# A gated recurrence of 512 steps: PSUM banks of equal width, and the state update as one scan over h, n, h

## The chip, the cores and the metric

The kernel runs on one core of a Trainium2 chip. The metric is the device time of one execution in microseconds (us); the time before is the median of three runs. The profile is of one further execution.

## The reference

A gated recurrent layer with a residual. For each of T = 512 steps, batch 8, width 512:

```python
def step(h, x_t):
    fused = jax.nn.sigmoid(jnp.concatenate([x_t, h], axis=-1) @ w_W + w_b)
    hidden_state, output_state = jnp.split(fused, 2, axis=-1)
    memory_state = x_t @ wx_W + wx_b + hidden_state * (h @ wh_W + wh_b)
    h_new = output_state * h + (1.0 - output_state) * jnp.tanh(memory_state)
    return (h_new, h_new)
```

The output is x plus all the h_new. In what follows r is `hidden_state`, z is `output_state`, hh is `h @ wh_W + wh_b`, n is the tanh. All is fp32. Each step needs h of the step before, so the 512 steps form one chain.

## The kernel before, in words

**Layout.** On TensorE the state is the stationary operand: a tile `hT` holds 128 partitions x 32 rows (4 steps of batch 8) for one of four k-blocks, and only the eight rows of the step at hand are not zero, so that four steps accumulate into one bank, each in its own rows. The 512 outputs are split into four strips j of 128 units, one to each 32-partition column strip of the array; within a strip the 128 units are half A (64) and half B (64). The width of a matmul is then the number of columns that a bank holds: hh, z and r of one half have 64 each. `hT` exists for each half, in eight buffers (`NH`); k-blocks 0 and 1 come from hTA, 2 and 3 from hTB.

**Banks.** Bank A has hh, z and r of half A (192 columns), Z has z of half B (64), B has r and hh of half B (128); each exists twice, one set for each group of four steps (`GS`). The share of x is computed a group ahead: one k-block of 384 columns in each step goes into `xp` ("prefill", `take(pre, 1)`), from where ScalarE copies the parts into the banks of the next group (`spread`), and VectorE turns x's share of the memory state (`turn_x`). `seed` copies the bias into `xp`. In the last eight steps there is no prefill.

**Order.** From the line `ctx.enter_context(tc.manual_schedule())` on, the instructions of each engine stand in the order in which the program writes them, and each engine works through its own in order. On TensorE that is `ORDER`, a letter for the bank and a digit for the k-block, four strips each, then the prefill block. A step of hTA can be used by A0, B0 and A1 ahead of hTB, which A2 is the first to need.

**The chain of a step.** VectorE turns 32 x 32 blocks from the bank (lines 232 for r and z, 244 for hh), ScalarE takes the sigmoid of the turned r into every second element of `md0`, hh and x's share alternate in `md1`, and one scan (line 264, state = d0 * state + d1) over pairs gives r * hh + x share in every second element of `m`. ScalarE takes the tanh of that into `hd1`, VectorE puts z * h beside it (line 275, `kept`), and the second scan (line 284, `update`), with 0 and 1 - z in `hd0`, gives (1 - z) * n + z * h into the `hT` of the next step. z and 1 - z are two sigmoids of the same turned values. GpSimd adds x to the new state and writes it to the output tile (line 315); sixteen steps make one transfer out.

On VectorE the order of a step is: turn r, hh, z of A, scan A, turn hh of B, `kept` of A, turn r of B, update A, turn z of B, scan B, `kept` of B, update B, `turn_x`. The wait for the release of an `hT` buffer by GpSimd, eight steps back, hangs on the transpose of hh of half A.

Of the kernel before, what the change touches and what calls it, by code (L numbers as in the profile page):

```python
# [7 lines left out]
F32 = mybir.dt.float32  # L8
AF = mybir.ActivationFunctionType
ALU = mybir.AluOpType  # L10
PSUM = bass.MemoryType.PSUM

P = 128
NQ = 4
GS = 4
B = 8
HU = 64


DVE_FILL = 4  # L20
SYNC = mybir.DependencyInfo(mybir.DependencyClass.Sync, mybir.DependencyReason.DATA)

ORDER = "A0 B0 A1 A2 A3 B1 B2 B3 Z0 Z1 Z2 Z3"

WH = {"A": slice(0, 192), "Z": slice(192, 256), "B": slice(256, 384)}

XP = {"A": slice(0, 192), "Z": slice(192, 256), "X": slice(256, 384), "B": slice(384, 512)}


@with_exitstack  # L30
def tile_cond_rnn_residual(
# [7 lines left out]
    out: bass.AP,  # L39
    TC: int,  # L40
):

# [18 lines left out]
    nc = tc.nc  # L63
    NCH = x.shape[0]
    T = NCH * TC
    NG = T // GS

    const = ctx.enter_context(tc.tile_pool(name="const", bufs=1))
# [7 lines left out]
    def load_x(c):  # L76
        if c < NCH:
            t_ = xin_p.tile([P, NQ, TC * B], F32, tag="xin", name=f"xin_{c}")
            nc.sync.dma_start(out=t_, in_=x[c].rearrange("p (k n) -> p k n", k=NQ))
            xins[c] = t_  # L80
# [7 lines left out]
    hin = const.tile([P, NQ, B], F32, name="hin")  # L88
# [8 lines left out]
    for k in range(NQ):  # L97
# [5 lines left out]

    NH = 2 * GS
    hT = [
        [const.tile([P, 32, 2, 2], F32, name=f"hT{n}{i}") for i in range(NH)]
        for n in "AB"
    ]

    md0 = [[const.tile([P, 32, 2, 2], F32, name=f"md0{n}{i}") for i in range(2)] for n in "AB"]  # L110
    md1 = [const.tile([P, 2, 32, 2, 2], F32, name=f"md1{i}") for i in range(2)]
    hd0 = [[const.tile([P, B, 2, 2], F32, name=f"hd0{n}{i}") for i in range(2)] for n in "AB"]
    hd1 = [[const.tile([P, B, 2, 2], F32, name=f"hd1{n}{i}") for i in range(2)] for n in "AB"]
    zs = [[const.tile([P, 2, B], F32, name=f"z{n}{i}") for i in range(2)] for n in "AB"]
    zeros = const.tile([P, 512], F32, name="zeros")
    nc.vector.memset(zeros, 0.0)
    for t_ in hT[0] + hT[1]:
        nc.gpsimd.memset(t_, 0.0)
    for n, t_ in enumerate(hd0[0] + hd0[1] + md0[0] + md0[1]):
        (nc.vector if n < DVE_FILL else nc.gpsimd).memset(t_, 0.0)  # L120

    def state(hf, i):

        s = i % GS
        return hT[hf][i % NH][:, B * s : B * s + B, :, 1]

    for hf in range(2):
        nc.vector.tensor_copy(
            state(hf, 0), hin[:, 2 * hf : 2 * hf + 2].rearrange("p c b -> p b c")
        )  # L130

    banks = [
        {n: psum.tile([P, c.stop - c.start], F32, name=f"{n}{q}") for n, c in WH.items()}
        for q in range(2)
    ]
    xps = [psum.tile([P, 512], F32, name=f"xp{q}") for q in range(2)]
# [12 lines left out]

    written = {}  # L150

    def act(key, *args, **kw):
        inst = nc.scalar.activation(*args, **kw).ins  # L153
        if key in written:
            tc.declare_no_dep(inst, written[key], reason="ordered through VectorE")
        written[key] = inst

    def seed(g):

        nc.scalar.copy(xps[g % 2], bias)  # L160
# [13 lines left out]
    def spread(g, names):  # L174

        for n in names:
            nc.scalar.copy(banks[g % 2][n], xps[g % 2][:, XP[n]])

    def turn_x(g, e):

        c0 = XP["X"].start + 32 * e
        nc.vector.transpose(
            md1[g % 2][:, e // 2, :, e % 2, 1], xps[g % 2][:, c0 : c0 + 32]
        )

    def take(it, n=None):
        while n is None or n > 0:
            if next(it, it) is it:
                return
            n = None if n is None else n - 1  # L190

    for g in range(2):
        seed(g)
        take(prefill(g))
        if g == 0:
            spread(0, "ABZ")
            for e in range(NQ):
                turn_x(0, e)
            seed(0)
    ctx.enter_context(tc.manual_schedule())  # L200

    pool_done = {}
    for i in range(T):
        g, s = divmod(i, GS)
        c, t = divmod(i, TC)
        ps = banks[g % 2]
        if t == 0:
            load_x(c + 3)
            ot = out_p.tile([P, NQ, TC, B], F32, tag="ot", name=f"ot_{c}")
        if s == 0:  # L210
            pre = prefill(g + 2) if g + 2 < NG else iter(())

        for n in ORDER.split():
            bank, k = n[0], int(n[1])
            hs = hT[k // 2][i % NH][:, :, k % 2, 1]
            for j in range(NQ):
                mm(ps[bank][32 * j : 32 * j + 32, :], hs, wh[:, k, j, WH[bank]])
        take(pre, 1)

        rows = slice(B * s, B * s + B)  # L220
        def flat(t_):
            return t_.rearrange("p n c s -> p (n c s)")

        raw = {
            "h": (ps["A"][:, :HU], ps["B"][:, HU:]),
            "z": (ps["A"][:, HU : 2 * HU], ps["Z"]),
            "r": (ps["A"][:, 2 * HU :], ps["B"][:, :HU]),
        }

        def turned(n, hf):  # L230
            t_ = work.tile([P, 2, 32], F32, tag=f"t{n}{hf}", name=f"t{n}{hf}_{i}")
            nc.vector.transpose(t_.rearrange("p c n -> p (c n)"), raw[n][hf])  # L232
            return t_[:, :, rows]

        def turn_r(hf):
            act(
                ("r", hf, g % 2, s),
                md0[hf][g % 2][:, rows, :, 1].rearrange("p n c -> p c n"),
                turned("r", hf),
                AF.Sigmoid,  # L240
            )

        def turn_h(hf):
            inst = nc.vector.transpose(  # L244
                md1[g % 2][:, hf, :, :, 0].rearrange("p n c -> p c n"), raw["h"][hf]
            ).ins

            if hf == 0 and i + 1 - NH in pool_done:
                tc.add_manual_dep(inst, pool_done[i + 1 - NH].name, SYNC)

        def turn_z(hf):
            tz = turned("z", hf)
            act(("z", hf, i % 2), zs[hf][i % 2], tz, AF.Sigmoid)
            act(
                ("zc", hf, i % 2),
                hd0[hf][i % 2][:, :, :, 1].rearrange("p n c -> p c n"),
                tz,
                AF.Sigmoid,
                scale=-1.0,
            )  # L260

        def memory(hf):
            m = work.tile([P, B, 2, 2], F32, tag=f"m{hf}", name=f"m{hf}_{i}")
            nc.vector.tensor_tensor_scan(  # L264
                flat(m),
                flat(md0[hf][g % 2][:, rows]),
                flat(md1[g % 2][:, hf, rows]),
                0.0,
                ALU.mult,
                ALU.add,  # L270
            )
            act(("n", hf, i % 2), hd1[hf][i % 2][:, :, :, 0], m[:, :, :, 1], AF.Tanh)

        def kept(hf):
            nc.vector.tensor_tensor(  # L275
                hd1[hf][i % 2][:, :, :, 1],
                zs[hf][i % 2].rearrange("p c n -> p n c"),
                state(hf, i),
                ALU.mult,
            )  # L280

        def update(hf):
            s1 = (i + 1) % GS
            nc.vector.tensor_tensor_scan(  # L284
                flat(hT[hf][(i + 1) % NH][:, B * s1 : B * s1 + B]),
                flat(hd0[hf][i % 2]),
                flat(hd1[hf][i % 2]),
                0.0,
                ALU.mult,
                ALU.add,  # L290
            )

        turn_r(0)
        turn_h(0)
        turn_z(0)
        memory(0)
        turn_h(1)
        kept(0)
        turn_r(1)
        update(0)  # L300
        turn_z(1)
        memory(1)
        kept(1)
        update(1)

        if g + 1 < NG:
            turn_x(g + 1, s)
            if s == 0:
                spread(g + 1, "A")
            elif s == 1:  # L310
                spread(g + 1, "BZ")
            elif s == 3 and g + 3 < NG:
                seed(g + 3)
        for hf in range(2):
            pool_done[i + 1] = nc.gpsimd.tensor_tensor(  # L315
                ot[:, 2 * hf : 2 * hf + 2, t, :].rearrange("p c n -> p n c"),
                xins[c][:, 2 * hf : 2 * hf + 2, t * B : t * B + B].rearrange("p c n -> p n c"),
                state(hf, i + 1),
                ALU.add,
            ).ins  # L320
        if t == TC - 1:
            nc.sync.dma_start(out=out[c], in_=ot.rearrange("p k t b -> p (k t b)"))
            xins.pop(c)
# [62 lines left out]
```

## Time and profile before

| | us |
|---|---|
| median of three runs (lowest, highest) | 1721.8 (1721.33, 1722.57) |
| profiled execution, its time | 1723.64 |
| profiled execution, its span | 1721.9 |
| PE busy (modelled ends) | 1707.1 |
| DVE busy | 1138.9 |
| ACT busy | 894.6 |
| POOL busy | 254.6 |

PE is TensorE, PEld its weight loads, DVE VectorE, ACT ScalarE, POOL GpSimd. A line of the timeline has the start in us from the span's start, the duration, the engine, the line of the code, the operation, output and inputs by the names of the program (buffer numbers left out), the shape, and how many were put together; in brackets the idle time before it, and what ended that. Loads of weights run ahead of the matmuls, so idle time before a load is not yet time lost. A matmul appears twice in the records[...]. Ends of matmuls are modelled; their starts are measured. In the tile view a line has the least, the median and the largest duration in ns, the first and last start, and the shape.

### The profile page before, as it was taken

Reading aid. Unit: us, or ns where it says so; the run is one execution under the profiler, and the core shown is the slowest. Engines: PE = TensorE matmul, PEld = TensorE weight load, DVE = VectorE, ACT = ScalarE, POOL = GpSimd, SP = SyncE. Lnnn points to the kernel's source line nnn. Section 1 sums busy time; section 2 is a strip of 40 time slices with the busy share of each in tenths; the row PEclk is TensorE's granted clock in tenths of the full one; section 3 lists DMA queues with packets and bytes.
Section 4 is the critical chain, followed back from the end, with each engine's and each line's share of the span. In section 5 each row is a group of like instructions: output and inputs, shape, how many; then the busy total and the mean of one; then the engine's idle time right before and its main releaser. Section 6 shows DMA issues by size and latency. Waiting matters only on the chain.

```text
span 1721.9 us, 121031 instructions
## 1 busy us (share of the span) xinstructions
PE 1707.1 (99%) x53312; PEld 1484.6 (86%) x53312; DVE 1138.9 (66%) x6663; ACT 894.6 (52%) x4610; POOL 254.6 (15%) x1048
## 2 busy tenths in 40 slices
PE   8999999999999999999999999999999999999998
PEld 5888888888888888888888888888888888888887
DVE  3666666666666666666666666666666666666666
ACT  3555555555555555555555555555555555555554
POOL 1111111111111111111111111111111111111111
PEclk9999999999999999999999999999999999999999
DMA  4000000000000000000000000000000000000000
GB/s 180 17 5 17 17 17 16 17 4 17 17 17 17 4 17 17 17 17 4 17 17 17 17 17 5 17 17 17 17 4 17 16 17 17 5 17 11 11 11 10
DMA packets 11232, 31.09 MB, mean 18 GB/s; under 512 B 1360, under 2 KB 1360, under 8 KB 10704
## 3 DMA queue, kind: packets, MB, share of 16 engines
q1 hardware_dynamic: 10368, 23.07, 3.9%
q8 instruction: 416, 6.82, 1.6%
q14 instruction: 112, 0.92, 0.2%
q10 hardware_dynamic: 336, 0.28, 0.1%
HBM read 14.96 MB, written 8.39 MB: 14 GB/s over the span
## 4 chain that ended last, share of the span: by engine, by line
PE 98%; DMA 1%; DVE 0%; issue 0%; ACT 0%; ACTq 0%; POOLq 0%; POOL 0%
PE A L139 39%; PE B L139 25%; PE xp L139 19%; PE Z L139 14%; DMA wh<-in_wh_dram 1%; DMA bias<-in_bias_dram 0%; DVE tr L232 0%; ACT md0A L153 0%; DVE hTA L284 0%; DVE m L264 0%; DVE md L244 0%; ACTq L85 0%; POOLq L380 0%; POOL ot L315 0%; DVE hd1A L275 0%
## 5 line engine op out<-in xcount | busy, mean ns | idle before, releaser
L139 PE MATMUL A<-wh,hTA 128*32 128x192 f32 x8192 | 554.0, 326 | 2.2 <-DVE hTA L284 2.2
L139 PEld LDWEIGHTS A<-wh,hTA 128*32 128x32 f32 x8192 | 319.3, 137 | 179.7 <-DVE hTA L284 178.4
L139 PE MATMUL A<-wh,hTB 128*32 128x192 f32 x8192 | 447.4, 327 | 2.0 <-DMA wh<-in_wh_dram 2.0
L139 PE MATMUL xp<-wx,xin 128*32 128x384 f32 x4096 | 444.9, 489 | 4.5 <-ACT xp L160 4.5
L139 PE MATMUL B<-wh,hTA 128*32 128x128 f32 x8192 | 449.3, 273 | 0.0
L232 DVE STREAM_TRANSPOSE tr<-A 128x64 f32<-128x64 f32 x512 | 128.0, 250 | 470.2 <-PE A L139 470.2
L153 ACT ACTIVATE md0A<-tr 128x16 f32<-128x16 f32 x512 | 121.1, 237 | 479.7 <-DVE tr L232 479.7
L139 PEld LDWEIGHTS B<-wh,hTA 128*32 128x32 f32 x8192 | 362.4, 136 | 2.0
L139 PE MATMUL B<-wh,hTB 128*32 128x128 f32 x8192 | 336.4, 273 | 0.0
L139 PEld LDWEIGHTS A<-wh,hTB 128*32 128x32 f32 x8192 | 300.4, 137 | 36.9 <-DMA wh<-in_wh_dram 1.6
L315 POOL TENSOR_TENSOR ot<-xin,hTA 128x16 f32<-128x16 f32 x512 | 126.3, 247 | 1115.6 <-DVE hTA L284 1032.9
L139 PEld LDWEIGHTS B<-wh,hTB 128*32 128x32 f32 x8192 | 266.3, 137 | 0.0
L139 PE MATMUL Z<-wh,hTB 128*32 128x64 f32 x8192 | 240.6, 226 | 0.0
L139 PE MATMUL Z<-wh,hTA 128*32 128x64 f32 x8192 | 234.6, 223 | 0.0
L139 PEld LDWEIGHTS Z<-wh,hTA 128*32 128x32 f32 x8192 | 218.3, 141 | 0.0
L139 PEld LDWEIGHTS Z<-wh,hTB 128*32 128x32 f32 x8192 | 200.1, 148 | 0.0
L315 POOL TENSOR_TENSOR ot<-xin,hTB 128x16 f32<-128x16 f32 x512 | 125.2, 245 | 348.1 <-DVE hTB L284 342.8
L153 ACT ACTIVATE md0B<-tr 128x16 f32<-128x16 f32 x512 | 119.1, 233 | 70.7 <-DVE tr L232 0.5
L284 DVE TENSOR_TENSOR_SCAN hTB<-hd0B,hd1B 128x32 f32<-128x32 f32 x512 | 115.1, 225 | 52.9
L264 DVE TENSOR_TENSOR_SCAN m<-md0B,md 128x32 f32<-128x32 f32 x512 | 147.7, 289 | 0.0
L244 DVE STREAM_TRANSPOSE md<-B 128x64 f32<-128x64 f32 x512 | 146.8, 287 | 0.0
L153 ACT ACTIVATE zB<-tz 128x16 f32<-128x16 f32 x512 | 110.8, 216 | 53.9
(42 smaller groups left out, 1860.5 us busy)
## 6 DMA issues: line engine op xcount, KB each, us to landing
xin<-in_x_dram SPq DMA_DIRECT2D x32, 256.0 KB, 3.0
out_dram<-ot SPq DMA_DIRECT2D x32, 256.0 KB, 2.0
wx<-in_wx_dram SPq DMA_DIRECT2D x4, 768.0 KB, 7.2
wh<-in_wh_dram SPq DMA_DIRECT2D x4, 768.0 KB, 11.3
bias<-in_bias_dram ACTq DMA_DIRECT2D x4, 64.0 KB, 5.1
hin<-in_h_dram ACTq DMA_DIRECT2D x1, 16.0 KB, 8.0
```

The source lines that it names most:

```text
L139: nc.tensor.matmul(out_, lhsT, rhs, start=start, stop=False, skip_group_check=True)
L153: inst = nc.scalar.activation(*args, **kw).ins
L232: nc.vector.transpose(t_.rearrange("p c n -> p (c n)"), raw[n][hf])
L244: inst = nc.vector.transpose(md1[g % 2][:, hf, :, :, 0].rearrange("p n c -> p c n"), raw["h"][hf]).ins
L264: nc.vector.tensor_tensor_scan(flat(m), flat(md0[hf][g % 2][:, rows]), flat(md1[g % 2][:, hf, rows]), 0.0, ALU.mult, ALU.add,)
L284: nc.vector.tensor_tensor_scan(flat(hT[hf][(i + 1) % NH][:, B * s1 : B * s1 + B]), flat(hd0[hf][i % 2]), flat(hd1[hf][i % 2]), 0.0, ALU.mu ...
L315: pool_done[i + 1] = nc.gpsimd.tensor_tensor(ot[:, 2 * hf : 2 * hf + 2, t, :].rearrange("p c n -> p n c"), xins[c][:, 2 * hf : 2 * hf + 2, ...
```

## The change

Three things are changed together.

- **Banks.** R has r of both halves, G has hh and z of half A, H has z and hh of half B, all of 128 columns. The order of TensorE becomes `R0 R1 G0 G1 R2 R3 G2 G3 H0 H1 H2 H3`: four blocks with hTA ahead of the first with hTB, and H last. The weights' columns are laid out to suit.
- **Update.** `hT` has three slots an element: h, n, h. The scan of `update` reads the `hT` of this step in this order with 0, -1 and 1 - z in `hd0`: it gives h, then n - h, then h + (1 - z)(n - h), and writes all three to the `hT` of the next step, whose third slot is the new state and what TensorE loads (a stride of three slots by two instead of two by two). The tanh goes to the second slot; ScalarE copies the new state to the first slot after the updates of both halves. `kept`, `hd1`, `zs` and the sigmoid of z are gone.
- **Order and waits.** VectorE turns r of both halves first, then works half A through to its update, then half B. The transpose of z waits for the sigmoid of r of its half (so the scan needs no wait on ScalarE of its own), and the wait for GpSimd's release moves to the transpose of r of half B. The copies into the next group's banks are one bank a step. Five memsets of one column each follow `turn_x` in each step. GpSimd's two additions of a step change places: half B's first. In the setup VectorE fills 15 tiles instead of 4; hT's fills join those shared with GpSimd.

In the built program, the first scan of a half waits for VectorE's own transpose alone, the update for ScalarE alone, GpSimd's addition of half B for VectorE, and that of half A for nothing further.

```diff
-DVE_FILL = 4
+DVE_FILL = 15
+IDLE = 5
-ORDER = "A0 B0 A1 A2 A3 B1 B2 B3 Z0 Z1 Z2 Z3"
+ORDER = "R0 R1 G0 G1 R2 R3 G2 G3 H0 H1 H2 H3"
-WH = {"A": slice(0, 192), "Z": slice(192, 256), "B": slice(256, 384)}
+WH = {"G": slice(0, 128), "R": slice(128, 256), "H": slice(256, 384)}
-XP = {"A": slice(0, 192), "Z": slice(192, 256), "X": slice(256, 384), "B": slice(384, 512)}
+XP = {"G": slice(0, 128), "R": slice(128, 256), "X": slice(256, 384), "H": slice(384, 512)}
...
-        [const.tile([P, 32, 2, 2], F32, name=f"hT{n}{i}") for i in range(NH)]
+        [const.tile([P, 32, 2, 3], F32, name=f"hT{n}{i}") for i in range(NH)]
...
-    md1 = [const.tile([P, 2, 32, 2, 2], F32, name=f"md1{i}") for i in range(2)]
-    hd0 = [[const.tile([P, B, 2, 2], F32, name=f"hd0{n}{i}") for i in range(2)] for n in "AB"]
-    hd1 = [[const.tile([P, B, 2, 2], F32, name=f"hd1{n}{i}") for i in range(2)] for n in "AB"]
-    zs = [[const.tile([P, 2, B], F32, name=f"z{n}{i}") for i in range(2)] for n in "AB"]
+    md1 = [[const.tile([P, 32, 2, 2], F32, name=f"md1{n}{i}") for i in range(2)] for n in "AB"]
+    hd0 = [[const.tile([P, B, 2, 3], F32, name=f"hd0{n}{i}") for i in range(2)] for n in "AB"]
...
-    for t_ in hT[0] + hT[1]:
-        nc.gpsimd.memset(t_, 0.0)
-    for n, t_ in enumerate(hd0[0] + hd0[1] + md0[0] + md0[1]):
+    for n, t_ in enumerate(hd0[0] + hd0[1] + md0[0] + md0[1] + hT[0] + hT[1]):
         (nc.vector if n < DVE_FILL else nc.gpsimd).memset(t_, 0.0)
+    for t_ in hd0[0] + hd0[1]:
+        nc.gpsimd.memset(t_[:, :, :, 1], -1.0)
+    idle = const.tile([P, IDLE], F32, name="idle")
...
-            hs = hT[k // 2][i % NH][:, :, k % 2, 1]
+            hs = hT[k // 2][i % NH][:, :, k % 2, 2]
...
-            "h": (ps["A"][:, :HU], ps["B"][:, HU:]),
-            "z": (ps["A"][:, HU : 2 * HU], ps["Z"]),
-            "r": (ps["A"][:, 2 * HU :], ps["B"][:, :HU]),
+            "h": (ps["G"][:, :HU], ps["H"][:, HU:]),
+            "z": (ps["G"][:, HU:], ps["H"][:, :HU]),
+            "r": (ps["R"][:, :HU], ps["R"][:, HU:]),
...
         def turn_r(hf):
-            act(
+            tr, inst = turned("r", hf)
+            if hf == 1 and i + 1 - NH in pool_done:
+                tc.add_manual_dep(inst, pool_done[i + 1 - NH].name, SYNC)
+            r_done[hf] = act(
                 ("r", hf, g % 2, s),
                 md0[hf][g % 2][:, rows, :, 1].rearrange("p n c -> p c n"),
-                turned("r", hf),
+                tr,
                 AF.Sigmoid,
             )
...
         def turn_z(hf):
-            tz = turned("z", hf)
-            act(("z", hf, i % 2), zs[hf][i % 2], tz, AF.Sigmoid)
+            tz, inst = turned("z", hf)
+            tc.add_manual_dep(inst, r_done[hf].name, SYNC)
             act(
                 ("zc", hf, i % 2),
-                hd0[hf][i % 2][:, :, :, 1].rearrange("p n c -> p c n"),
+                hd0[hf][i % 2][:, :, :, 2].rearrange("p n c -> p c n"),
                 tz,
                 AF.Sigmoid,
                 scale=-1.0,
...
-            act(("n", hf, i % 2), hd1[hf][i % 2][:, :, :, 0], m[:, :, :, 1], AF.Tanh)
-
-        def kept(hf):
-            nc.vector.tensor_tensor(
-                hd1[hf][i % 2][:, :, :, 1],
-                zs[hf][i % 2].rearrange("p c n -> p n c"),
-                state(hf, i),
-                ALU.mult,
-            )
+            act(("n", hf, i % NH), state(hf, i, 1), m[:, :, :, 1], AF.Tanh)
...
                 flat(hd0[hf][i % 2]),
-                flat(hd1[hf][i % 2]),
+                flat(hT[hf][i % NH][:, rows]),
...
         turn_r(0)
+        turn_r(1)
         turn_h(0)
         turn_z(0)
         memory(0)
+        update(0)
         turn_h(1)
-        kept(0)
-        turn_r(1)
-        update(0)
         turn_z(1)
         memory(1)
-        kept(1)
         update(1)
+        for hf in range(2):
+            act(("h", hf, (i + 1) % NH), state(hf, i + 1, 0), state(hf, i + 1), AF.Copy)
 
         if g + 1 < NG:
             turn_x(g + 1, s)
-            if s == 0:
-                spread(g + 1, "A")
-            elif s == 1:
-                spread(g + 1, "BZ")
-            elif s == 3 and g + 3 < NG:
+            if s < 3:
+                spread(g + 1, "RGH"[s])
+            elif g + 3 < NG:
                 seed(g + 3)
-        for hf in range(2):
+        for n in range(IDLE):
+            nc.vector.memset(idle[:, n : n + 1], 0.0)
+        for hf in (1, 0):
             pool_done[i + 1] = nc.gpsimd.tensor_tensor(
```

More of the change, by code (lines that the diff above doesn't have):

```diff
@@ L110, in tile_cond_rnn_residual, with state @@
     md0 = [[const.tile([P, 32, 2, 2], F32, name=f"md0{n}{i}") for i in range(2)] for n in "AB"]
-    md1 = [const.tile([P, 2, 32, 2, 2], F32, name=f"md1{i}") for i in range(2)]
-    hd0 = [[const.tile([P, B, 2, 2], F32, name=f"hd0{n}{i}") for i in range(2)] for n in "AB"]
-    hd1 = [[const.tile([P, B, 2, 2], F32, name=f"hd1{n}{i}") for i in range(2)] for n in "AB"]
-    zs = [[const.tile([P, 2, B], F32, name=f"z{n}{i}") for i in range(2)] for n in "AB"]
+    md1 = [[const.tile([P, 32, 2, 2], F32, name=f"md1{n}{i}") for i in range(2)] for n in "AB"]
+    hd0 = [[const.tile([P, B, 2, 3], F32, name=f"hd0{n}{i}") for i in range(2)] for n in "AB"]
     zeros = const.tile([P, 512], F32, name="zeros")
     nc.vector.memset(zeros, 0.0)
-    for t_ in hT[0] + hT[1]:
-        nc.gpsimd.memset(t_, 0.0)
-    for n, t_ in enumerate(hd0[0] + hd0[1] + md0[0] + md0[1]):
+    for n, t_ in enumerate(hd0[0] + hd0[1] + md0[0] + md0[1] + hT[0] + hT[1]):
         (nc.vector if n < DVE_FILL else nc.gpsimd).memset(t_, 0.0)
-    def state(hf, i):
+    for t_ in hd0[0] + hd0[1]:
+        nc.gpsimd.memset(t_[:, :, :, 1], -1.0)
+    idle = const.tile([P, IDLE], F32, name="idle")
+    def state(hf, i, slot=2):
         s = i % GS
-        return hT[hf][i % NH][:, B * s : B * s + B, :, 1]
+        return hT[hf][i % NH][:, B * s : B * s + B, :, slot]
     for hf in range(2):
-        nc.vector.tensor_copy(
-            state(hf, 0), hin[:, 2 * hf : 2 * hf + 2].rearrange("p c b -> p b c")
-        )
+        for slot in (0, 2):
+            nc.vector.tensor_copy(
+                state(hf, 0, slot), hin[:, 2 * hf : 2 * hf + 2].rearrange("p c b -> p b c")
+            )
     banks = [
@@ L150, in tile_cond_rnn_residual, with act @@
     written = {}
-    def act(key, *args, **kw):
-        inst = nc.scalar.activation(*args, **kw).ins
+    def act(key, out_, in_, func, **kw):
+        inst = nc.scalar.activation(out_, in_, func, **kw).ins
         if key in written:
@@ L156, in act @@
         written[key] = inst
+        return inst
     def seed(g):
@@ L182, in turn_x @@
         nc.vector.transpose(
-            md1[g % 2][:, e // 2, :, e % 2, 1], xps[g % 2][:, c0 : c0 + 32]
+            md1[e // 2][g % 2][:, :, e % 2, 1], xps[g % 2][:, c0 : c0 + 32]
         )
@@ L195, in tile_cond_rnn_residual @@
         if g == 0:
-            spread(0, "ABZ")
+            spread(0, "RGH")
             for e in range(NQ):
@@ L231, in turned @@
             t_ = work.tile([P, 2, 32], F32, tag=f"t{n}{hf}", name=f"t{n}{hf}_{i}")
-            nc.vector.transpose(t_.rearrange("p c n -> p (c n)"), raw[n][hf])
-            return t_[:, :, rows]
+            inst = nc.vector.transpose(t_.rearrange("p c n -> p (c n)"), raw[n][hf]).ins
+            return t_[:, :, rows], inst
+        r_done = [None, None]
         def turn_r(hf):
-            act(
+            tr, inst = turned("r", hf)
+            if hf == 1 and i + 1 - NH in pool_done:
+                tc.add_manual_dep(inst, pool_done[i + 1 - NH].name, SYNC)
+            r_done[hf] = act(
                 ("r", hf, g % 2, s),
                 md0[hf][g % 2][:, rows, :, 1].rearrange("p n c -> p c n"),
-                turned("r", hf),
+                tr,
                 AF.Sigmoid,
@@ L243, in turn_h @@
         def turn_h(hf):
[L244 to L249, printed above, removed]
+            nc.vector.transpose(
+                md1[hf][g % 2][:, :, :, 0].rearrange("p n c -> p c n"), raw["h"][hf]
+            )
         def turn_z(hf):
-            tz = turned("z", hf)
-            act(("z", hf, i % 2), zs[hf][i % 2], tz, AF.Sigmoid)
+            tz, inst = turned("z", hf)
+            tc.add_manual_dep(inst, r_done[hf].name, SYNC)
             act(
                 ("zc", hf, i % 2),
-                hd0[hf][i % 2][:, :, :, 1].rearrange("p n c -> p c n"),
+                hd0[hf][i % 2][:, :, :, 2].rearrange("p n c -> p c n"),
                 tz,
@@ L266, in memory @@
                 flat(md0[hf][g % 2][:, rows]),
-                flat(md1[g % 2][:, hf, rows]),
+                flat(md1[hf][g % 2][:, rows]),
                 0.0,
@@ L271, in memory @@
             )
-            act(("n", hf, i % 2), hd1[hf][i % 2][:, :, :, 0], m[:, :, :, 1], AF.Tanh)
-        def kept(hf):
-            nc.vector.tensor_tensor(
-                hd1[hf][i % 2][:, :, :, 1],
-                zs[hf][i % 2].rearrange("p c n -> p n c"),
-                state(hf, i),
-                ALU.mult,
-            )
+            act(("n", hf, i % NH), state(hf, i, 1), m[:, :, :, 1], AF.Tanh)
         def update(hf):
@@ L359 @@
     r, z = w[:, :512], w[:, 512:]
-    wx_d = c_(units(cat((z[:D], half_a), (r[:D], half_a), (z[:D], half_b), (wxm, both), (r[:D], half_b))))
-    wh_d = c_(units(cat((whm, half_a), (z[D:], half_a), (r[D:], half_a), (z[D:], half_b), (r[D:], half_b), (whm, half_b))))
+    wx_d = c_(units(cat((z[:D], half_a), (r[:D], both), (wxm, both), (z[:D], half_b))))
+    wh_d = c_(units(cat((whm, half_a), (z[D:], half_a), (r[D:], both), (z[D:], half_b), (whm, half_b))))
     rb, zb = wb[:512], wb[512:]
-    bias_d = c_(cat((whb, half_a), (zb, half_a), (rb, half_a), (zb, half_b), (wxb, both), (rb, half_b), (whb, half_b))[0])
+    bias_d = c_(cat((whb, half_a), (zb, half_a), (rb, both), (wxb, both), (zb, half_b), (whb, half_b))[0])
     xd = units(_np.moveaxis(x, 2, 0))
```

## The prediction

> **What bounds the kernel now.** First the page's busy shares and its chain that ended last:
>
> ```profile
> PE 1707.1 (99%) x53312; PEld 1484.6 (86%) x53312; DVE 1138.9 (66%) x6663; ACT 894.6 (52%) x4610; POOL 254.6 (15%) x1048
> PE 98%; DMA 1%; DVE 0%; issue 0%; ACT 0%; ACTq 0%; POOLq 0%; POOL 0%
> ```
>
> TensorE looks like the only bound. But ends of matmuls are modelled, so I went to the timeline of one step in mid-run and read starts alone:
>
> ```profile
> 900.48 0.43 PE L139 MATMUL B<-wh,hTA 128*32 128x128 f32 x8
> 900.70 0.65 PE L139 MATMUL B<-wh,hTB 128*32 128x128 f32 x16
> 900.74 0.25 DVE L232 STREAM_TRANSPOSE tr<-A 128x64 f32<-128x64 f32 x1 [0.91 <-PE A L139]
> 900.92 0.26 DVE L244 STREAM_TRANSPOSE md<-A 128x64 f32<-128x64 f32 x1
> 901.13 0.45 PE L139 MATMUL Z<-wh,hTA 128*32 128x64 f32 x16
> 901.62 0.85 PE L139 MATMUL xp<-wx,xin 128*32 128x384 f32 x8
> 902.13 0.32 PEld L139 LDWEIGHTS A<-wh,hTA 128*32 128x32 f32 x8 [0.35 <-DVE hTA L284]
> 902.27 0.53 PE L139 MATMUL A<-wh,hTA 128*32 128x192 f32 x8
> 902.78 0.22 DVE L284 TENSOR_TENSOR_SCAN hTB<-hd0B,hd1B 128x32 f32<-128x32 f32 x1
> 903.06 0.26 PEld L139 LDWEIGHTS A<-wh,hTB 128*32 128x32 f32 x8
> 903.14 0.37 PE L139 MATMUL A<-wh,hTB 128*32 128x192 f32 x4
> ```
>
> A k-block is eight matmul records: four column strips side by side, two passes. Starts give 0.325 us for a block of 192 columns, 0.218 for 128 (901.13 - 900.48 is three), 0.122 for Z's 64 (0.49 for four), 0.645 for the prefill block: 4 x 0.325 + 4 x 0.218 + 4 x 0.122 + 0.645 = 3.306 us. The median pitch of all steps in the trace is 3.307. So TensorE sets the step, yet with little to spare: the first weight load of hTB is released at 903.06, and its matmul goes at 903.14. A step without a prefill block shows what lies right below:
>
> ```profile
> 1706.16 0.40 PE L139 MATMUL B<-wh,hTA 128*32 128x128 f32 x8
> 1706.41 0.25 DVE L232 STREAM_TRANSPOSE tr<-A 128x64 f32<-128x64 f32 x1 [0.88 <-PE A L139]
> 1707.10 0.28 DVE L244 STREAM_TRANSPOSE md<-B 128x64 f32<-128x64 f32 x1
> 1707.52 0.22 DVE L284 TENSOR_TENSOR_SCAN hTA<-hd0A,hd1A 128x32 f32<-128x32 f32 x1
> 1707.79 0.56 PE L139 MATMUL A<-wh,hTA 128*32 128x192 f32 x8 [0.31 <-DVE hTA L284]
> 1708.44 0.22 DVE L284 TENSOR_TENSOR_SCAN hTB<-hd0B,hd1B 128x32 f32<-128x32 f32 x1
> 1708.72 0.38 PEld L139 LDWEIGHTS A<-wh,hTB 128*32 128x32 f32 x12 [0.17 <-DVE hTB L284]
> ```
>
> Here TensorE has 2.66 us of work and waits for both states, and the last steps still come every 3.267 us (A's transposes at 1706.41, 1709.68, 1712.94). That is the loop through VectorE: bank A done, half A, half B, hTB, A2, A3. It hides under 3.307 by 40 ns. Any change of order has to be judged on that loop as well as on TensorE's sum.
>
> [...] half B's scan, which starts just after GpSimd's addition of hTA, is lengthened, half A's is not.
>
> ```profile
> L264 DVE TENSOR_TENSOR_SCAN m<-md0A,md x512: 223/225/230, 23.9 to 1716.8; 128x32 f32<-128x32 f32 x171
> L264 DVE TENSOR_TENSOR_SCAN m<-md0B,md x512: 224/293/308, 24.8 to 1717.6; 128x32 f32<-128x32 f32 x171
> ```
>
> **The change, part by part.** Gaps below are medians over the steps of the trace.
>
> *Banks.* Twelve blocks of 128 columns and the prefill: 12 x 0.218 + 0.645 = 3.266 us, 41 ns less. Z's blocks took 0.122 although the other widths (0.645, 0.325, 0.218: some 1.68 ns a column and 2.5 ns a pass) put 64 columns at 0.111; that excess goes. The weights are read at a stride of 24 bytes and not 16, which no row shows. Z loaded eight sets in 0.122 us; the new blocks have 0.218, so a load could be 78% slower unseen. I take nothing.
>
> *ScalarE.* The two z sigmoids of a step (217 and 216 ns) go, two copies of h come, of the tanh's shape (220). They stand behind both tanhs, and the next sigmoid comes over a microsecond later; the copied slot is needed a whole step later. What queues behind the copy that waits for hTB is a bank copy (250) or the bias copy (591): hTB's end + 34 + some 130 + 591 is still some 300 ns ahead of the next r transposes' results. Nothing. Without that cover, up to 0.2 us a step.
>
> *VectorE.* Two products leave (154 and 177), five one-column memsets come (the 128x32 memset of the setup takes 85; 0.4 us at most for five). They sit between the turn of x and the r transposes, a stretch of some 0.8 us: hidden. If they aren't, the r transposes are late by what sticks out.
>
> *GpSimd.* Its additions now both follow hTB, half B first, some 0.57 us after hTB's end in all. [...] half B's scan should fall back from 293 to 225: -68. The transfer of a finished output tile goes some 0.25 us later, once each sixteen steps and at the end: 0.25 us. The slot's release waits eight steps: hidden.
>
> *The loop.* New order on VectorE: r of A, r of B, h of A, z of A, scan A, update A, h of B, z of B, scan B, update B. Let 0 be the moment when the last column of G has gone in (first H matmul). In ns:
> - h of A starts at 251: bank A to its transpose is 250 in the tail (1706.16 to 1706.41), 260 to 273 in mid-run.
> - Scan A needs this transpose complete. It lasts 266 when not first after a wait; the first after a wait is longer (tr 250, tz 206, same shape), so I take 294; bounds 266 and 312. VectorE sees its own completion 38 later (seen on the waits of updates). Scan A starts at 581.
> - Scan 225, to ScalarE 34, tanh 221, back 32: 512. Update A starts at 1093. (Before, this last step took 55 to 76, because the update carried two waits or stood behind a transpose.)
> - The update scans 48 elements instead of 32[...]. It lasts 257 and holds VectorE for 174 (the 32-element one 141). H has been ready for VectorE since 874 + 251 = 1125; its transpose starts at 1093 + 174 = 1267, so it stands 142 behind the update of A.
> - It lasts 286 (half B's row), + 36: scan B at 1589. + 512: update B at 2101, ends 2358.
> - Weight load 53 later, and the first matmul 55 longer than normal (380 against 326 in the trace): R2 effectively starts at 2466.
> - R2, R3, G2, G3: 4 x 218.5 = 874. The loop closes at 3340.
>
> TensorE alone would start R2 at H (874) + prefill (645) + R0, R1, G0, G1 (874) = 2393. So it waits 73 ns in every step. Half A is in time: update A ends at 1350, + 108 = 1458, against 1519 needed.
>
> Against before: TensorE's blocks give 41 back; the loop, which had been 40 under the bound, is now 74 over the new one. Why longer, though the sigmoid of r is off it? h, z of A and both of B now wait for later banks: before, A3 closed with B1 to B3, Z and the prefill still to come, and half B's h and r came from a bank finished 0.49 us ahead of Z. Now h and z of B arrive in the last bank, and all of half B's chain hangs behind it.
>
> *Sum.* 504 steps x (3340 - 3307) = 16.6 us; 8 steps without prefill x (3340 - 3267) = 0.6; end 0.25. Setup: the same 24 fills, sixteen of them half as large again, and four small ones, all under the first transfers (the first step starts at 17.6 us): nothing. 1721.9 + 17.4 = **1739** for the profiled span. That execution took 1723.6, its span is within 0.1 of the runs' median (1721.8), so the same difference goes on the median: 1739.
>
> **Rivals.**
> 1. *TensorE stays the bound.* If the first transpose after a wait costs no more (-28), the drain of the last matmul is 10 shorter, the longer scan holds the engine no longer than the short one (-33), and the transpose of B takes 269 as A's does (-17), then 88 ns are gone where 74 would do, and the step is 3.266: 1722 - 504 x 0.041 = 1701. This is the other side of my forecast; it begins to be faster than before where the loop is over 33 ns shorter than I have it. For it: 33 ns is 1% of ten summed terms. Against it: each term would have to be at its low end.
> 2. *Even.* The loop comes out within 7 ns of 3307: 1718 to 1725.
> 3. *A second queue sticks out.* z of A also waits for A's r sigmoid: R done + 251 + 250 + 34 + 236 + 32 = 803, that is 366 after G, against its own turn at 425: 59 to spare. Should the memsets be held up behind GpSimd's additions (570 ns) and only then take 85 each, the r transposes would be late by up to 0.2 us and the loop by up to 0.14: 1739 + 504 x 0.14 = 1810.[...]
> 4. *The copies don't stay hidden*, and the next sigmoid is late by 20 to 50 ns beyond its spare: 1750 to 1765. The order on ScalarE speaks against it.
>
> **Chances.** Forecast 0.63, own range 1726 to 1755 (sums of the terms' bounds, -25 and +32 ns a step). Rival 1 and what lies between it and even 0.21; even 0.08; rivals 3 and 4 together 0.08. Range 1702 to 1757: it cuts off the lower part of rival 1 and the upper of 3. The runs of before spread by 0.07%; 0.2% is about what can be told from no change. Faster 0.21, same 0.08, slower 0.71.
>
> **What would show it.** Right: pitch of a step near 3.34 us in mid-run and in the tail alike; the weight load of R from hTB released by update B with its matmul right on it and 380 or so minus the narrower width long, step after step; R from hTA not waiting; the update at 257; half B's scan back at 225; h of B starting some 174 after update A. Wrong: pitch 3.266 with the load ahead of its matmul by more than 55 ns (rival 1), or the r transposes starting after a memset and not after TensorE (rival 3), or z of A released by ScalarE. The longest unproven terms are the 294 and the 174.

## The result, and the profile after

| | before | changed |
|---|---|---|
| median of four runs, us (lowest, highest) | 1722.03 (1721.33, 1722.57) | 1749.2 (1748.49, 1750.64) |
| ratio, 95% interval | | 1.0159 (1.0141 to 1.0177) |
| span of the profiled execution, us | 1721.9 | 1746.7 |
| median pitch of a step, ns | 3307 | 3362 |
| pitch in the last steps, without prefill, ns | 3267 | 3355 |

The pitch is the time from the start of one step to the start of the next. The changed kernel is slower by 27 us, where 17 were forecast, with 1702 to 1757 as the range. The profile says where it comes from. First, of the page of the changed kernel, the two lines that the prediction shows of the page before:

```profile
PE 1732.3 (99%) x53312; PEld 1454.8 (83%) x53312; DVE 1070.4 (61%) x8212; ACT 929.0 (53%) x4610; POOL 230.9 (13%) x1041
PE 98%; DMA 1%; DVE 0%; issue 0%; ACT 0%; ACTq 0%; POOL 0%; POOLq 0%
```

VectorE does 69 us less, TensorE's matmuls are the same work, and yet TensorE is "99% busy" for 25 us longer. That points to a wait hidden in the modelled ends. The timeline of one step in mid-run:

```profile
900.19 0.62 PE L143 MATMUL H<-wh,hTA 128*32 128x128 f32 x16
900.44 0.32 DVE L255 STREAM_TRANSPOSE md1A<-G 128x64 f32<-128x64 f32 x1
900.79 0.22 DVE L273 TENSOR_TENSOR_SCAN m<-md0A,md1A 128x32 f32<-128x32 f32 x1
901.31 0.26 DVE L285 TENSOR_TENSOR_SCAN hTA<-hd0A,hTA 128x48 f32<-128x48 f32 x1 [0.29 <-ACT hTA L157]
901.48 0.28 DVE L255 STREAM_TRANSPOSE md1B<-H 128x64 f32<-128x64 f32 x1
901.62 0.47 PEld L143 LDWEIGHTS R<-wh,hTA 128*32 128x32 f32 x16 [0.42 <-DVE hTA L285]
901.71 0.62 PE L143 MATMUL R<-wh,hTA 128*32 128x128 f32 x16
901.80 0.23 DVE L273 TENSOR_TENSOR_SCAN m<-md0B,md1B 128x32 f32<-128x32 f32 x1
902.15 0.62 PE L143 MATMUL G<-wh,hTA 128*32 128x128 f32 x16
902.32 0.26 DVE L285 TENSOR_TENSOR_SCAN hTB<-hd0B,hTB 128x48 f32<-128x48 f32 x1 [0.29 <-ACT hTB L157]
902.63 0.43 PEld L143 LDWEIGHTS R<-wh,hTB 128*32 128x32 f32 x16
902.63 0.67 PE L143 MATMUL R<-wh,hTB 128*32 128x128 f32 x16
```

Read the two waits of TensorE's loads. The first, R from hTA, has idle time before it (0.42), and still its matmul goes at 901.71, 0.09 behind the load, where the prefill's stream ends: nothing is lost. The second, R from hTB, has no idle time named in this view, and loses: the matmuls of G from hTA begin at 902.15 and would end their stream 0.437 later, at 902.58 or 902.59; load and matmul start together at 902.63, and the first matmul then takes 50 ns longer than usual. The groups of matmuls show the same in their means, and the group of the loads that wait shows idle time:

```profile
L143 PE MATMUL R<-wh,hTB 128*32 128x128 f32 x8192 | 344.2, 285 | 1.6 <-DMA wh<-in_wh_dram 1.6
L143 PE MATMUL R<-wh,hTA 128*32 128x128 f32 x8192 | 318.0, 273 | 2.6 <-DVE hTA L285 2.6
L143 PE MATMUL G<-wh,hTB 128*32 128x128 f32 x8192 | 317.6, 273 | 0.0
L143 PEld LDWEIGHTS R<-wh,hTB 128*32 128x32 f32 x8192 | 219.6, 139 | 56.8 <-DMA wh<-in_wh_dram 1.6
```

The means are 285 against 273 in equal shapes, and the matmuls have no idle time but 1.6 us at the start. The loads of R from hTB have 56.8 us of it, 0.11 us in each step; for nearly all of that the page names no releaser, so the line of the matmuls' means is the plainer sign. The pitch is 3362, TensorE's blocks alone are 3266: 96 ns of waiting in each step.

The last steps, without prefill, nearly keep the pitch (3355), as they should if a loop through VectorE sets the step and not TensorE's work; there half A is late as well, and it makes no difference:

```profile
1728.76 0.67 PE L143 MATMUL R<-wh,hTA 128*32 128x128 f32 x16 [0.37 <-DVE hTA L285]
1729.77 0.67 PE L143 MATMUL R<-wh,hTB 128*32 128x128 f32 x16
1732.11 0.67 PE L143 MATMUL R<-wh,hTA 128*32 128x128 f32 x16 [0.36 <-DVE hTA L285]
```

1732.11 - 1728.76 is 3.35. Last, the tile view of the scans' input and output: half B's scan is back at 225, and the transpose of h of A takes 314.

```profile
L255 DVE STREAM_TRANSPOSE md1A<-G x512: 306/314/321, 22.1 to 1741.0; 128x64 f32<-128x64 f32 x171
L273 DVE TENSOR_TENSOR_SCAN m<-md0A,md1A x512: 224/225/228, 22.5 to 1741.4; 128x32 f32<-128x32 f32 x171
L273 DVE TENSOR_TENSOR_SCAN m<-md0B,md1B x512: 224/225/228, 23.6 to 1742.3; 128x32 f32<-128x32 f32 x171
```

### The profile page after: what moved, and what is told of

Same layout as the page of the kernel before. It is cut to its first block, busy times and chain, and to the rows that moved or that the text cites. A ratio compares the mean times of both kernels' runs of the same rounds, so it can differ in the third digit from the quotient of the medians.

```text
span 1746.7 us, 121040 instructions
## 1 busy us (share of the span) xinstructions
PE 1732.3 (99%) x53312; PEld 1454.8 (83%) x53312; DVE 1070.4 (61%) x8212; ACT 929.0 (53%) x4610; POOL 230.9 (13%) x1041
## 4 chain that ended last, share of the span: by engine, by line
PE 98%; DMA 1%; DVE 0%; issue 0%; ACT 0%; ACTq 0%; POOL 0%; POOLq 0%
PE R L143 28%; PE G L143 26%; PE H L143 25%; PE xp L143 19%; DMA wh<-in_wh_dram 1%; DMA bias<-in_bias_dram 0%; DVE md1A L255 0%; DVE hTA L285 0%; ACT hd0A L157 0%; ACT hTA L157 0%; ACTq L89 0%; POOL ot L316 0%; DVE tz L237 0%; POOLq L381 0%; DVE hTB L285 0%
## 5 line engine op out<-in xcount | busy, mean ns | idle before, releaser
L143 PE MATMUL R<-wh,hTB 128*32 128x128 f32 x8192 | 344.2, 285 | 1.6 <-DMA wh<-in_wh_dram 1.6
L143 PE MATMUL R<-wh,hTA 128*32 128x128 f32 x8192 | 318.0, 273 | 2.6 <-DVE hTA L285 2.6
L143 PE MATMUL G<-wh,hTB 128*32 128x128 f32 x8192 | 317.6, 273 | 0.0
L143 PE MATMUL H<-wh,hTB 128*32 128x128 f32 x8192 | 317.6, 273 | 0.0
L143 PE MATMUL G<-wh,hTA 128*32 128x128 f32 x8192 | 317.6, 273 | 0.0
L143 PE MATMUL H<-wh,hTA 128*32 128x128 f32 x8192 | 317.6, 273 | 0.0
L143 PEld LDWEIGHTS R<-wh,hTB 128*32 128x32 f32 x8192 | 219.6, 139 | 56.8 <-DMA wh<-in_wh_dram 1.6
L143 PEld LDWEIGHTS H<-wh,hTA 128*32 128x32 f32 x8192 | 247.7, 136 | 0.0
L143 PEld LDWEIGHTS H<-wh,hTB 128*32 128x32 f32 x8192 | 247.5, 136 | 0.0
L143 PEld LDWEIGHTS G<-wh,hTB 128*32 128x32 f32 x8192 | 247.3, 136 | 0.0
L143 PEld LDWEIGHTS G<-wh,hTA 128*32 128x32 f32 x8192 | 247.1, 136 | 0.0
```

Source lines behind the costliest of these rows:

```text
L143: nc.tensor.matmul(out_, lhsT, rhs, start=start, stop=False, skip_group_check=True)
```

## The experiments

**1 and 2. Which state is late?** Theory: half B's newest state sets the step through one loop. The rivals are TensorE itself (other widths, other stride of its loads) and half A. Each half in turn is loaded from the step before, which leaves out the recurrence through the newest state of that half; all instructions stay. These two runs and the two of experiments 3 and 4 are one execution each.

```diff
-            hs = hT[k // 2][i % NH][:, :, k % 2, 2]
+            hs = hT[k // 2][(i - k // 2) % NH][:, :, k % 2, 2]       # stale_b
+            hs = hT[k // 2][(i - 1 + k // 2) % NH][:, :, k % 2, 2]   # stale_a
```

> The changed kernel, but k-blocks 2 and 3 load the hTB of one step earlier, so TensorE never waits for half B's newest state (the recurrence through half B is left out; all instructions stay). Theory (the loop through half B's update sets the step): the step falls from 3.36 to TensorE's own 3.27 us, the time from 1749 to about 1700. Rival 'TensorE itself is slower with the new banks or with loads at a stride of 24 bytes': the time stays at 1749. Rival 'half A's chain is late too': it stays between, above 1710.

Measured: 1699.9, a pitch of 3265.

> The changed kernel, but k-blocks 0 and 1 load the hTA of one step earlier (the recurrence through half A's newest state is left out). Theory: half A is in time by some 60 ns, so nothing changes: 1749, within 4 us. Rival 'half A's chain is the late one': the time falls towards 1700.

Measured: 1752.3, a pitch of 3363. In the run with the older hTB the timeline shows hTB's update at the same place of a step, but the matmul that uses R now goes on without it, at the end of G's stream:

```profile
900.96 0.62 PE L143 MATMUL G<-wh,hTA 128*32 128x128 f32 x16
901.13 0.26 DVE L285 TENSOR_TENSOR_SCAN hTB<-hd0B,hTB 128x48 f32<-128x48 f32 x1 [0.29 <-ACT hTB L157]
901.29 0.49 PEld L143 LDWEIGHTS R<-wh,hTB 128*32 128x32 f32 x16
901.39 0.62 PE L143 MATMUL R<-wh,hTB 128*32 128x128 f32 x16
```

The whole of the 96 ns hangs on half B. TensorE's own sum is what the prediction had (3266), so narrower banks and the stride of 24 bytes cost nothing that can be told; half A is in time, for here its newest state is still used.

**3 and 4. Is it the chain, or VectorE's work?** The same additional transpose, in two places of VectorE's order. Nobody reads its output.

```diff
         update(0)
+        extra()        # x_on_path:  nc.vector.transpose of H's z columns
         turn_h(1)
...
         update(1)
+        extra()        # x_off_path
```

> One transpose of H's z columns more in each step (to a tile nobody reads), on VectorE between the update of A and the transpose of h of B. It holds VectorE for about 131 ns. Theory: all of half B's chain moves by it: 512 x 0.131 = 67 us, 1816. Rival 'TensorE is the bound, VectorE is only 61% busy': no more than a few us.

Measured: 1819.0, pitch 3496: +134 ns a step.

> The same additional transpose, but after the update of B, ahead of the turn of x. Theory: it lies in VectorE's spare stretch before the r transposes: 1749, within 4 us. Rival 'VectorE's sum of work counts, or the r transposes are already late': up to 67 us more, as on the path.

Measured: 1751.5, pitch 3366. One operation costs 134 ns in the one place and at most 4 in the other. This is what "on the loop" means, and VectorE's 61% of busy time says nothing about it.

**5. Is the longer scan to blame?** Banks and orders as changed, but the update of before: n and z * h in pairs, 32 elements. Some of the edit:

```diff
             tc.add_manual_dep(inst, r_done[hf].name, SYNC)
+            act(("z", hf, i % 2), zs[hf][i % 2], tz, AF.Sigmoid)
             act(("zc", hf, i % 2), ...
...
-            act(("n", hf, i % NH), state(hf, i, 1), m[:, :, :, 1], AF.Tanh)
+            act(("n", hf, i % 2), hd1[hf][i % 2][:, :, :, 0], m[:, :, :, 1], AF.Tanh)
...
         memory(0)
+        kept(0)
         update(0)
```

> The changed banks and orders with the update of before: pairs of n and z * h, 32 elements a scan, both sigmoids of z, the product on VectorE ahead of the update, no copies. Theory: the scan is 33 ns shorter on each half, but the second sigmoid of z stands in front of each tanh (about +55 and +59 ns) and the update carries two waits (+23 each): the loop is about 93 ns longer, 1796. Rival 'the scan of 48 elements is what made the changed kernel slow': 1749 - 512 x 0.066 = 1715.

Measured: 1808.2, ratio to the kernel before 1.0492 (1.0477 to 1.0508); pitch 3461, 99 ns more than with the scan of 48. The step grows about as expected (93 were), the way there isn't quite the expected one. Medians from the moment when G is done: the tanh of A starts at 893 (858 in the changed kernel) and ends at 1095 (1083). The product that goes beside it has to wait for z's sigmoid, which ends at 882; it starts at 914 and ends at 1091. The update needs both and carries a wait as an instruction of its own; it starts at 1194, 99 ns after the tanh's end, where the changed kernel has 32 and starts at 1115. The two inputs end within 4 ns of each other, so the trace doesn't tell which of them the update waits for. The timeline:

```profile
902.91 0.22 ACT L157 ACTIVATE zA<-tz 128x16 f32<-128x16 f32 x1 [0.20 <-DVE tz L237]
903.14 0.21 ACT L157 ACTIVATE hd1A<-m 128x16 f32<-128x16 f32 x1
903.16 0.18 DVE L285 TENSOR_TENSOR hd1A<-zA,hTA 128x16 f32<-128x16 f32 x1
903.44 0.22 DVE L294 TENSOR_TENSOR_SCAN hTA<-hd0A,hd1A 128x32 f32<-128x32 f32 x1
```

So the longer scan is not to blame: of the three parts of the change the new update is the good one, and with these banks and this order it saves some 50 us. (8 us of the difference is another thing, told under the hardware.) The other two parts, taken together and with the old update, are 85 us slower than the kernel before; experiment 8 keeps the widths of the banks and changes what they hold and when.

**6. The memsets.** `IDLE = 0`.

> The changed kernel without the five one-column memsets of a step. Theory: they lie in a spare stretch, 1749 within 3 us. Rival 'they delay the r transposes': faster by 5 us or more.

Measured: 1751.9, ratio 1.0166 (1.0151 to 1.0181) against 1.0159 (1.0141 to 1.0177) with them. They aren't what delays the changed kernel; without them it is no faster.

**7. GpSimd's order.** `for hf in (0, 1)` instead of `(1, 0)`.

> The changed kernel with GpSimd's two additions of a step in the order of before: half A's first, which then starts some 80 ns after update A ends (about 1.45 us after G is done, for 0.25 us), while half B's scan starts at 1.61. Theory [...] (there the scan of half B started 25 ns after the addition and took 293 and not 225 ns, ending 71 ns after the addition): here the addition ends 90 ns after the scan starts, so the scan would end at 1.77 even if held, and it ends at 1.83 by itself: 1749 within 3 us, half B's scan at 225. Rival 'any overlap lengthens the scan by 68 ns or more': 1749 + 512 x 0.068 = 1784.

Measured: 1750.6, ratio 1.0165 (1.0148 to 1.0182); half B's scan stays at 225, although it overlaps with the addition:

```profile
903.06 0.25 POOL L316 TENSOR_TENSOR ot<-xin,hTA 128x16 f32<-128x16 f32 x1 [2.11 <-DVE hTA L285]
903.23 0.22 DVE L273 TENSOR_TENSOR_SCAN m<-md0B,md1B 128x32 f32<-128x32 f32 x1
```

In the kernel before the scan started 25 ns after the addition and was 68 ns longer; here it starts 170 ns after it and is not. So this overlap with GpSimd's addition does not lengthen the scan; what lengthened it in the kernel before (293 against 225) was not shown. The new order of the two additions was not needed: half B's scan falls back to 225 in either order, with its later place behind the update of A.

**8. A version that beats both.** If the loop is too long from "hTB loaded" to "VectorE begins", fewer blocks should stand there. Widths stay at 128, contents change: G = hh and r of A, R = z of A and r of B, H = z and hh of B.

```diff
-ORDER = "R0 R1 G0 G1 R2 R3 G2 G3 H0 H1 H2 H3"
+ORDER = "G0 G1 R0 R1 G2 G3 R2 R3 H0 H1 H2 H3"
...
-            "z": (ps["G"][:, HU:], ps["H"][:, :HU]),
-            "r": (ps["R"][:, :HU], ps["R"][:, HU:]),
+            "z": (ps["R"][:, :HU], ps["H"][:, :HU]),
+            "r": (ps["G"][:, HU:], ps["R"][:, HU:]),
...
         turn_r(0)
-        turn_r(1)
         turn_h(0)
         turn_z(0)
         memory(0)
+        turn_r(1)
         update(0)
```

The columns of the weights and the copies into the banks follow; the transpose of z of A no longer waits for the sigmoid of r.

> The changed kernel with other contents of the banks, widths as before (128): G has hh and r of half A, R has z of A and r of B, H stays z and hh of B. TensorE's order is G0 G1 R0 R1, then G2 G3 R2 R3, H0 to H3; VectorE's is r, hh, z and scan of A, r of B, update A, half B. Theory: hTB is now followed by two blocks (437 ns) before VectorE can begin, where there were four (874); the sigmoid of r comes onto the loop (scan A some 900 ns after G is done, where it was 600). Summed: the loop wants R2's place 2.79 us after G is done, TensorE gets there at 2.83: TensorE bound, 3.27 us a step, 1701 us, faster than both kernels. Rival 'some other wait takes over, such as z of A waiting for its bank': 1715 to 1750.

Measured: 1699.3 (1698.94 to 1700.61), ratio to the kernel before 0.9863 (0.9846 to 0.9879), 24 us less than before and 50 less than the changed kernel; pitch 3264.

```profile
900.21 0.62 PE L143 MATMUL G<-wh,hTB 128*32 128x128 f32 x16
900.90 0.25 DVE L237 STREAM_TRANSPOSE tr<-G 128x64 f32<-128x64 f32 x1 [0.68 <-PE G L143]
902.21 0.31 DVE L255 STREAM_TRANSPOSE md1B<-H 128x64 f32<-128x64 f32 x1
903.08 0.26 DVE L286 TENSOR_TENSOR_SCAN hTB<-hd0B,hTB 128x48 f32<-128x48 f32 x1 [0.30 <-ACT hTB L157]
903.39 0.35 PEld L143 LDWEIGHTS G<-wh,hTB 128*32 128x32 f32 x10
903.48 0.39 PE L143 MATMUL G<-wh,hTB 128*32 128x128 f32 x6
```

The load is released at 903.39, the matmul follows at 903.48 at the end of R's stream (903.04 + 0.437): 90 ns between them. In the changed kernel, where load and matmul start together, the matmul takes 50 ns longer; if those 50 are what a load needs ahead of its matmul, an estimate, hTB is in time by about 40. TensorE is the bound, at the 3266 that the banks of 128 columns promised. The price of the regrouping is on VectorE: from the transpose at which the loop enters it (r of A here, h of A in the changed kernel) to the end of hTB's update it takes 2431 ns instead of 2132, since the sigmoid of r is on the loop now. Two blocks less are 437 ns, so the loop is some 138 shorter in all; the last steps, without prefill, come every 3227 (3355 in the changed kernel).

**9 and 10. Late steps.** Two more runs, one execution each, belong to an observation told under the hardware, late starts whole multiples of 128 VectorE instructions apart: `IDLE = 1` with the update of before, and `IDLE = 4` with the regrouped banks.

> The run with the update of before, with one memset a step and not five, so that VectorE has 16 instructions a step (waits of their own counted) and not 20. In the run with 20 every 32nd step came 0.35 us late and every 32nd another 0.18, where one VectorE instruction started late though nothing it waits for was. Theory[...]: 128 is eight steps of 16[...]; the late steps of the 32-step pattern go, and either none is late (span 1797) or each eighth one is (512 / 8 x 0.18 to 0.35 = 11 to 22 us more). Rival 'the late steps have to do with the data or the transfers': the same 32 late steps, 1805.

Measured: span 1797.5 (time 1799.3), and past the first ten steps none is late by more than 30 ns.

> The regrouped banks with four memsets a step and not five: 16 VectorE instructions a step and not 17. With 17 four steps were 0.25 us late, 128 steps apart (128 x 17 = 17 x 128). [...] no step late at a distance of 128; none at all (span about 1696) or each eighth (some 16 us more).

Measured: span 1696.2 (time 1698.0); past the first ten steps none is late by more than 30 ns.

## Why the prediction was right, point by point

**The bound and the gain in TensorE.** 3266 ns a step, 41 less than before: 3265 in the run with the older hTB, 3264 with the regrouped banks. Right.

**The loop.** Every step of the sum can be laid beside the medians of the trace, counted from the moment when G is done:

| starts, ns | predicted | measured |
|---|---|---|
| transpose of h of A | 251 | 250 |
| scan A | 581 | 599 |
| update A | 1093 | 1115 |
| transpose of h of B | 1267 | 1290 |
| scan B | 1589 | 1606 |
| update B | 2101 | 2125 |
| update B ends | 2358 | 2383 |
| R from hTB, effectively | 2466 | 2488 |
| G done again | 3340 | 3362 |

The 22 ns that are missing come from one term, the first transpose. The prediction said "I take 294; bounds 266 and 312": it takes 314, a little over the upper bound. Its own lines would have given it nearly all: 250 against 206 for equal shapes are 44 for the first after a wait, and 266 + 44 is 310; it took 28. The other terms cancel within 5 ns. The scan of 48 elements was put at 257 and its hold on VectorE at 174, the author's estimates, which no trace of before shows; measured were 258 and 175.

Two sums are off in print by less than that: 251 + 294 + 38 is 583 and not 581, and 12 x 0.218 + 0.645 is 3.261 as printed; with the 218.5 ns that stand further down it is 3.267, and 3265 was measured. Half A is in time, but with less to spare than forecast: its update ends at 1373, + 108 = 1481, against 1518 needed, so 37 ns and not 61.

**From the step to the time.** 504 x 55 + 8 x 88 ns are 28.4 us; the two profiles differ by 24.8. The mean pitch rose less than the median (3312.8 to 3363.3), because the kernel before had more single late steps (3855, 3825 and 3605 the longest past the start) than the changed one, which had none off by over 25 ns; and the first step came 1.2 us earlier. The medians of the runs differ by 27.2. At 1749 the time lies inside the prediction's own range of 1726 to 1755, towards its upper end.

**The hidden parts.** ScalarE's two copies, VectorE's memsets, GpSimd's later additions: right. The copies start at 1989 and 2417, the next sigmoid of r 1.0 us later. The five memsets start within some 25 ns of each other, far from the 0.4 us that was allowed for them (rival 3); taking them out changed nothing that can be told. The wait of z of A for r's sigmoid cost nothing: that sigmoid ends at 332, and z's transpose starts at 424, 174 after the one of h.

**Half B's scan at 225** was right; the reason given for it, that GpSimd's additions change places, was not: experiment 7 has the old order and 225 as well.

**Rival 1**, TensorE as the bound, needed 74 ns off the loop; the runs show 96. It came true in the regrouped version only.

## What to carry to other kernels

In a recurrence cut into halves, write down the loop from "newest state loaded" round to itself as one sum, with each engine's order in it, beside the sum of the busiest engine. In these runs the step was the larger of the two (3362 against 3266 in the changed kernel; 3266 against a loop of some 3227 in the regrouped one), and "99% busy" stood on the page of both. Here what shortened that loop was not a smaller operation but fewer blocks between the arrival of the late half and the first thing that needs it: the same widths, regrouped, turned 1.6% slower into 1.4% faster. And the wait of 96 ns a step in the changed kernel shows no idle time at its matmuls past 1.6 us at the start, and at its loads 56.8 us, for nearly all of which no releaser is named: look for a load and its matmul that start together (both at 902.63), and for a matmul group whose mean exceeds that of its equals (285 against 273).

## What the runs showed of the hardware

**In these runs a transpose from a bank that began after VectorE stood waiting was 43 to 48 ns longer, and the one that writes every fourth element was some 60 longer.** With the regrouped banks z's transpose, which writes its elements side by side, has a median of 207 when it follows another one and 251 when it is the first after a wait; that of h, of the same shape, writes every fourth element and takes 266 and 309 (314 in the changed kernel). In the changed kernel z's transpose of A starts 174 after that of h, the first after a wait; behind h of A in the kernel before, which follows another transpose, the next instruction starts 131 later. The four of one step:

```profile
901.07 0.27 DVE L255 STREAM_TRANSPOSE md1A<-G 128x64 f32<-128x64 f32 x1
901.34 0.25 DVE L237 STREAM_TRANSPOSE tz<-R 128x64 f32<-128x64 f32 x1
902.21 0.31 DVE L255 STREAM_TRANSPOSE md1B<-H 128x64 f32<-128x64 f32 x1
902.38 0.21 DVE L237 STREAM_TRANSPOSE tz<-H 128x64 f32<-128x64 f32 x1
```

**Some of VectorE's instructions came late.** In the run with the update of before (experiment 5), steps 14, 46, 78 and so on, counted from 0, came 0.35 us late, and 27, 59, 91 came 0.18 late. Here is hTB's update, with the product ahead of it, in a step that is on time and in step 238:

```profile
900.76 0.18 DVE L285 TENSOR_TENSOR hd1B<-zB,hTB 128x16 f32<-128x16 f32 x1
901.04 0.23 DVE L294 TENSOR_TENSOR_SCAN hTB<-hd0B,hd1B 128x32 f32<-128x32 f32 x1
851.77 0.18 DVE L285 TENSOR_TENSOR hd1B<-zB,hTB 128x16 f32<-128x16 f32 x1
852.40 0.22 DVE L294 TENSOR_TENSOR_SCAN hTB<-hd0B,hd1B 128x32 f32<-128x32 f32 x1 [0.46 <-ACT hd1B L157]
```

In step 238 everything is on time up to the wait in front of the update, and the update itself starts 350 ns late, with nothing outstanding that the profile shows. The kernel has 20 VectorE instructions a step, waits of their own counted. Two regularities:

- The late steps repeat after 32 steps with 20 instructions a step (32 x 20 = 5 x 128) and after 128 steps with 17, in the regrouped kernel (128 x 17 = 17 x 128).
- Count VectorE's instructions through the trace, waits of their own too. In steps 10 to 503, the starts that are over 40 ns behind their usual distance from the instruction ahead are 46 with 20 instructions a step and 8 with the regrouped banks (17 a step), and those of one run all lie a whole multiple of 128 instructions apart.

Why an instruction is late at these places the traces do not show.

With 16 a step, 128 instructions are eight whole steps. In both kernels tried (9 and 10) the late steps were gone. In the one the span fell by 8.1 us (1805.6 to 1797.5), where the late steps had added up to 8.5; in the other it fell by 1.0, which is what its four had added up to, but no more than executions of one kernel differ. Not every kernel is like that: the run with the additional transpose on the loop has 17 a step and no such late step, and the run with the older hTA has 16, and in it one step in 24 is 57 ns late. The changed kernel has 16 as well, with its five memsets. That this is what the memsets are good for was not shown; without them (11 a step) a few steps were late by some 50 ns, and the time was the same within what can be told.
